# Two 3x3 convolutions of a metaformer block: where the batch statistics are taken, how the rectification is spread, and in which order three engines work in the second one

## The chip, the cores and the metric

The kernel runs on one core of a Trainium2 chip. The metric is the time of one execution on the device in microseconds (us). The core's engines work side by side, each through a queue of its own: TensorE (PE: matmuls), VectorE (DVE), ScalarE (ACT), GpSimd (POOL) and SyncE (SP, here only a queue for DMA). They wait for one another by semaphores. The two on-chip memories are SBUF and PSUM; matmuls write PSUM.

## The reference, cut to what matters

The program is a two-layer network on an image of 2 x 256 x 56 x 56 (batch, channels, rows, columns). Layer 0 is attention in windows and a mixture of experts. Layer 1 starts with this residual block of convolutions, and ends with a second mixture of experts. The change is in the block alone:

```python
def noised_tri_conv(x, w):
    tq = ternary_quantize(w - jnp.mean(w))          # -1, 0 or 1
    out = lax.conv_general_dilated(x, tq, (1, 1), ((1, 1), (1, 1)), ...)   # 3x3, 256 -> 256
    center = tq[:, :, 1, 1]
    return out + jnp.einsum('bchw,oc->bohw', x, center)

def batch_norm_train(x, gamma, beta):
    mean = jnp.mean(x, axis=(0, 2, 3), keepdims=True)
    var = jnp.var(x, axis=(0, 2, 3), keepdims=True)
    return (x - mean) * lax.rsqrt(var + BN_EPS) * gamma[...] + beta[...]

out1 = jax.nn.relu(batch_norm_train(noised_tri_conv(x, w1), g1, b1))
out2 = batch_norm_train(noised_tri_conv(out1, w2), g2, b2)
return jax.nn.relu(out1 + out2)
```

The mean and the variance go over the whole image of each channel. So nothing of `out1` can be rectified before the first convolution has ended everywhere, and nothing after the second can start before all its statistics are there.

## The kernel before, in words

**Tiling.** The image is cut into 14 strips of 8 rows (`STRIPS`, 7 per batch element; `SR` = 8, `NT` = 448 = 8 x 56). The channels lie on the 128 partitions in two halves (`KC` = 2; index `k` for the input's, `o` for the output's). `x_all` holds the results of all strips, `pad[b]` holds the padded input of one batch element, to which `inner(b, s)` and `narrow` give views.

**First convolution, `conv` (from line 1906).** It works on units of two strips. Rows are combined in pairs so that four products (`c`) with combined weights give two rows at once. `component(u, c)` makes the combined input `v` (VectorE for the first unit, GpSimd after it), ScalarE rounds it to `hi`, and VectorE makes the rest `lo = v - hi` (line 1903); both go through TensorE with the same weights, 12 matmuls of 448 columns for each `o` (line 1928). The results are summed into `x_all` by lines 1947 to 1954, and after the last product (c = 3) `bn_stats` takes the statistics of the two strips, one instruction each (line 1956).

**Affine.** `affine` aggregates the statistics with `bn_aggr` (line 2106) and makes a scale and a shift per channel. `between(i)` (line 2164 and around) rectifies strip i on ScalarE into `pad`, one instruction for each `o`.

**Second convolution, `conv43` (from line 1980).** It works on units of four strips, the first of two (`FOURS` = (0,1), (2-5), (6-9), (10-13)). Six products per unit (c = 0 to 5) give four rows at once. `component(u, c)` makes the combined input in PSUM (`pv`) out of helper tiles: p and q for c = 1 and 2, r and s for c = 3 and 4, a new r for c = 0, a new s for c = 5; r and s have one buffer each. For c = 3 the first unit makes r and s on VectorE, the later ones on GpSimd (`eng`, lines 2024 and 2025). ScalarE casts `hi` out of `pv` (line 2038) and VectorE makes `lo` (line 2039). A product has 12 matmuls for each `o` (line 2071), of 448 columns, of 224 in the first unit, into one of four PSUM banks (`pc`). ScalarE copies the results of c = 1 and 3 into `x_all` (line 2081), VectorE adds and subtracts those of c = 2 and 4 (lines 2084 and 2085), and adds those of c = 0 and 5 to rows 0 and 3 (lines 2087 and 2089). After c = 4, seven operations of GpSimd and ScalarE mix the four rows (lines 2093 to 2099: y0 += y2, y3 *= 2, y2 *= 3, y1 += y3, y2 += y0, y3 *= 3, y3 += y1). After c = 5, `bn_stats` takes the statistics strip by strip (line 2091), four instructions per `o`.

**What sets the order.** The order of the products is a list written out by hand (`steps`): (0,1) to (0,4), then for each next unit u: (u,1), (u-1,0), (u,2), (u-1,5), (u,3), (u,4); at the end (3,0), (3,5). In the source, the input of product n + 2 is made ahead of the matmuls of product n. `at_step` is called at the head of every product; `rectifying` then rectifies at c = 1 all strips of the next unit and one beyond, and strips 0 to 2 ahead of everything. Source order is the order on an engine only inside `tc.manual_schedule(engines=...)`. In `conv` that holds SP alone, in `conv43` no engine; there a planner in the compiler sets the order of each engine's queue from its own estimates. `ENGINES` is SP, DVE, PE and ACT, without POOL.

The next stage (`all_strips`, `residual`, from line 2203) needs scale2 and shift2.

Of the kernel before, what the change touches and what calls it, by code (L numbers as in the profile page):

```python
# [1 line left out]

# [1 line left out]

# [6 lines left out]
F32 = mybir.dt.float32  # L11
# [632 lines left out]
def metaformer(ctx: ExitStack, tc: tile.TileContext, a: dict, out: bass.AP, flag):  # L644
# [1199 lines left out]
    with mid:  # L1844

        with ExitStack() as st:
# [59 lines left out]
            def conv(sums, at_step):  # L1906
# [10 lines left out]
                for n, (u, c) in enumerate(steps):  # L1917
                    at_step(n)
                    if n + 2 < len(steps):
                        parts.append(component(*steps[n + 2]))  # L1920
                    hi, lo = parts.pop(0)
                    for o in range(KC):
                        pc = ps.tile([P, 512], F32, tag="cv", name="pc")
                        m = 0
                        for k in range(KC):
                            for dx in range(3):
                                for part in (hi, lo):
                                    nc.tensor.matmul(  # L1928
                                        pc[:, :NT],
                                        wq[:, k, c, dx * C + o * P : dx * C + (o + 1) * P],  # L1930
                                        part[:, :, k, dx : dx + W],
                                        start=m == 0,
                                        stop=m == 2 * KC * 3 - 1,
                                    )
                                    m += 1
                        pc = pc[:, :NT]

                        def row(y):
                            r = x_all[:, 2 * u : 2 * u + 2, o * NT : (o + 1) * NT]
                            r = r.rearrange("p s (h w) -> p s h w", w=W)[:, :, y : SR - 1 + y : 2, :]  # L1940
                            return r

                        def rows(ap):
                            return ap.rearrange("p (s h w) -> p s h w", s=2, w=W)

                        if c == 1:
                            nc.scalar.copy(row(1), rows(pc))
                        elif c == 2:
                            nc.vector.tensor_tensor(row(0), row(1), rows(pc), ALU.add)
                            nc.vector.tensor_tensor(row(1), row(1), rows(pc), ALU.subtract)  # L1950
                        elif c == 0:
                            nc.vector.tensor_tensor(row(0), row(0), rows(pc), ALU.add)
                        else:
                            nc.vector.tensor_tensor(row(1), row(1), rows(pc), ALU.subtract)
                            for i in (2 * u, 2 * u + 1):
                                nc.vector.bn_stats(stats[:, o, i, :], X[STRIPS[i]][:, o, :])
                return stats

            def weights43(taps):
# [20 lines left out]
            def conv43(wq, cp, vps, tp, at_step):  # L1980
# [6 lines left out]
                def component(u, c):  # L1987
# [7 lines left out]
                        else:  # L1995
                            runs.append([2 * (i - strips[0]), b, s * SR, 2])
                    n = 2 * len(strips)
                    eng = nc.gpsimd if u else nc.vector

                    def on_rows(op):  # L2000
                        for at, b, y, m in runs:
                            d = [pad[b][:, y + q : y + q + 4 * m - 3 : 4] for q in range(6)]
                            op(slice(at, at + m), d)
# [17 lines left out]
                        nc.vector.tensor_tensor(v, banks(p), banks(q), ALU.subtract)  # L2021
                    elif c == 3:
                        p, q = kept["r", u], kept["s", u] = tile_of("r", bufs=1), tile_of("s", bufs=1)
                        on_rows(lambda at, d: eng.tensor_tensor(p[:, at], d[4], d[2], ALU.subtract))
                        on_rows(lambda at, d: eng.tensor_tensor(q[:, at], d[3], d[1], ALU.subtract))
# [14 lines left out]
                    return hi, lo  # L2040

                stats = tp.tile([P, KC, len(STRIPS), 6], F32, tag="stats4", name="stats4")
                steps = [(0, c) for c in (1, 2, 3, 4)]
                for u in range(1, len(FOURS)):
                    steps += [(u, 1), (u - 1, 0), (u, 2), (u - 1, 5), (u, 3), (u, 4)]
                steps += [(len(FOURS) - 1, c) for c in (0, 5)]
                at_step(-1, 1)
                parts = [component(*steps[n]) for n in range(2)]
                for n, (u, c) in enumerate(steps):
# [8 lines left out]
                    def row(y, o):  # L2058
                        r = wide[:, :, o * NT : (o + 1) * NT]
                        return r.rearrange("p s (g q w) -> p s g q w", q=4, w=W)[:, :, :, y, :]  # L2060

                    def both(y):
                        return wide.rearrange("p s (g q w) -> p s g q w", q=4, w=W)[:, :, :, y, :]

                    for o in range(KC):
                        pc = ps.tile([P, 512], F32, tag="cv", name="pc")
                        m = 0
# [18 lines left out]
                        elif c == 0:  # L2086
                            nc.vector.tensor_tensor(row(0, o), row(0, o), got, ALU.add)
                        else:
                            nc.vector.tensor_tensor(row(3, o), row(3, o), got, ALU.add)
                            for i in strips:  # L2090
                                nc.vector.bn_stats(stats[:, o, i, :], X[STRIPS[i]][:, o, :])
                    if c == 4:
                        nc.gpsimd.tensor_tensor(both(0), both(0), both(2), ALU.add)
                        nc.scalar.mul(both(3), both(3), 2.0)
                        nc.scalar.mul(both(2), both(2), 3.0)
                        nc.gpsimd.tensor_tensor(both(1), both(1), both(3), ALU.add)
                        nc.gpsimd.tensor_tensor(both(2), both(2), both(0), ALU.add)
                        nc.scalar.mul(both(3), both(3), 3.0)
                        nc.gpsimd.tensor_tensor(both(3), both(3), both(1), ALU.add)
                return stats  # L2100

            def affine(stats, g, beta, tp, eps=eps5):

                mv = tp.tile([P, KC, 2], F32, tag="mv", name="mv")
                for o in range(KC):
                    nc.vector.bn_aggr(mv[:, o, :], stats[:, o].rearrange("p s c -> p (s c)"))
# [44 lines left out]

            with tc.manual_schedule(engines={mybir.EngineType.SP}):
                stats = conv(sums[0], combining)
            scale, shift = affine(stats, bn["g1"], bn["b1"], rp)
# [4 lines left out]
            def between(i):  # L2159
# [3 lines left out]
                for o in range(KC):  # L2163
# [17 lines left out]
        wq_held.close()  # L2181

        with ExitStack() as both:
# [335 lines left out]
```

## Time and profile before

| what | value |
|---|---|
| time, median of 3 runs | 1740.41 us (1736.08 to 1745.44) |
| time of the profiled execution | 1737.13 us |
| its span in the trace | 1735.3 us |
| busy in the span | PE 87%, DVE 55%, ACT 40%, POOL 37% |
| first convolution, matmuls of line 1928 start | 817.6 to 994.9 us |
| second convolution, matmuls of line 2071 start | 1004.6 to 1129.0 us |
| first transposes of the next stage | 1137.8 us |

Engines in three stretches (busy us; "clock" is the TensorE clock that was granted, as a share of full speed):

| stretch, us | PE | DVE | ACT | POOL | clock |
|---|---|---|---|---|---|
| 1025 to 1052 | 27.0 | 25.9 | 9.0 | 10.1 | 0.98 |
| 1052 to 1084 | 31.3 | 25.5 | 9.8 | 13.8 | 1.00 |
| 1084 to 1129 | 41.4 | 31.5 | 12.6 | 20.6 | 1.00 |

How to read the lines of the profile: a line of the timeline has the start in us, the duration in us, engine, line of the code, operation, output <- inputs with partitions x elements, and how many were merged; in brackets the engine's idle time before it and what ended it. A line of a group has line, engine, operation, count | busy us, mean ns | idle time before, and what ended most of it. "PE busy" counts a matmul from start to modelled end; as matmuls overlap, the time that one takes from the engine is read from the distance between starts.

### The profile page before, as it was taken

Reading aid. Unit: us, or ns where it says so; the run is one execution under the profiler, and the core shown is the slowest. Engines: PE = TensorE matmul, PEld = TensorE weight load, DVE = VectorE, ACT = ScalarE, POOL = GpSimd, SP = SyncE. Lnnn points to the kernel's source line nnn. Section 1 sums busy time; section 2 is a strip of 40 time slices with the busy share of each in tenths; the row PEclk is TensorE's granted clock in tenths of the full one; section 3 lists DMA queues with packets and bytes.
Section 4 is the critical chain, followed back from the end, with each engine's and each line's share of the span. In section 5 each row is a group of like instructions: output and inputs, shape, how many; then the busy total and the mean of one; then the engine's idle time right before and its main releaser. Section 6 shows DMA issues by size and latency. Waiting matters only on the chain. (4 is left out here: it accounts for less than half of the span.)

```text
span 1735.3 us, 25573 instructions
## 1 busy us (share of the span) xinstructions
PE 1507.6 (87%) x8445; PEld 1176.0 (68%) x8445; DVE 957.5 (55%) x2620; ACT 692.9 (40%) x1419; POOL 636.8 (37%) x728
## 2 busy tenths in 40 slices
PE   5999998999878788894989879957769999999964
PEld 3555565556557667783768768746658888888852
DVE  3456667466635335885999888777622212111136
ACT  2544443444323324544444263235423334343323
POOL 2111436235333653552333323427715542222210
PEclk9999999999879999996999989955579999999975
DMA  7112334112257769794441000024357777888858
GB/s 241 42 64 90 111 102 145 60 62 80 80 181 248 249 203 322 258 331 176 170 170 70 1 1 0 10 65 141 126 198 274 271 258 262 282 288 288 293 198 317
DMA packets 94157, 291.78 MB, mean 168 GB/s; under 512 B 20151, under 2 KB 35611, under 8 KB 84928
## 3 DMA queue, kind: packets, MB, share of 16 engines
q1 hardware_dynamic: 70384, 231.82, 40.3%
q0 software_dynamic: 19824, 51.82, 7.9%
q10 hardware_dynamic: 3808, 6.42, 1.0%
q8 instruction: 69, 1.13, 0.3%
q14 instruction: 72, 0.59, 0.1%
HBM read 218.55 MB, written 74.20 MB: 169 GB/s over the span
## 5 line engine op out<-in xcount | busy, mean ns | idle before, releaser
L1187 PE MATMUL ph<-ut,w 128*128 128x256 f32 (+1 forms) x1472 | 311.8, 363 | 18.5 <-DMA w<-in_L_experts 10.0
L1216 DVE TENSOR_TENSOR y<-py,w 128x512 f32<-128x512 f32 (+1 forms) x120 | 76.8, 640 | 412.5 <-PE py L1206 341.4
L1206 PE MATMUL py<-w,h 128*128 128x256 f32 x1288 | 300.5, 381 | 3.4 <-DVE y L1216 2.5
L1187 PEld LDWEIGHTS ph<-ut,w 128*128 128x128 f32 x1472 | 251.4, 195 | 49.6 <-DMA w<-in_L_experts 10.3
L1206 PEld LDWEIGHTS py<-w,h 128*128 128x128 f32 x1288 | 244.5, 192 | 37.1 <-DVE y L1216 2.9
L934 POOL DMA_INDIRECT xs<-u,pos x196 | 194.0, 990 | 127.9 <-issue 43.1
L1218 POOL DMA_INDIRECT ys<-y,dest x136 | 137.0, 1008 | 233.0 <-DVE dest L1162 100.4
L1194 ACT ACTIVATE h<-ph,w 128x256 f32<-128x256 f32 (+1 forms) x368 | 162.6, 448 | 119.0 <-PE ph L1187 91.5
L1597 ACT ACTIVATE ex<-sc 112x476 f32<-112x476 f32 (+3 forms) x224 | 116.9, 573 | 177.6 <-PE sc L1587 169.8
L1159 ACT COPY ut<-pt 128x512 f32<-128x512 f32 (+1 forms) x120 | 65.1, 543 | 293.1 <-PE pt L1155 258.2
L1928 PE MATMUL pc<-lo,wq 128*128 128x448 f32 x336 | 131.8, 394 | 5.7 <-DVE lo L1903 5.4
L1617 DVE TENSOR_TENSOR acc<-av,acc 128x238 f32<-128x238 f32 (+3 forms) x224 | 88.1, 408 | 82.9 <-PE av L1607 74.7
L1928 PE MATMUL pc<-hi,wq 128*128 128x448 f32 x336 | 131.0, 392 | 2.5 <-DVE x L1950 1.9
L1607 PE MATMUL av<-ex,vals 112*64 112x238 f32 (+3 forms) x896 | 126.9, 407 | 4.0 <-DVE acc L1617 4.0
L1218 POOL DMA_INDIRECT ys<-y,to x81 | 81.7, 1009 | 121.9 <-DVE dest L1162 63.4
L2071 PE MATMUL pc<-hi,wq 128*128 128x448 f32 (+1 forms) x288 | 102.5, 366 | 18.1 <-ACT hi L2038 9.4
L1578 PE MATMUL sc<-q_im,keys 32*112 32x238 f32 (+3 forms) x896 | 99.2, 423 | 7.9 <-ACT ex L1597 7.8
L2071 PE MATMUL pc<-lo,wq 128*128 128x448 f32 (+1 forms) x288 | 101.8, 363 | 0.2 <-DVE lo L2039 0.2
L1155 PE MATMUL pt<-ident,xg 128*128 128x128 f32 x434 | 71.2, 285 | 33.6 <-DMA xg<-xs 25.5
L1901 POOL TENSOR_TENSOR v<-pad 128x928 f32<-128x928 f32 (+1 forms) x28 | 56.7, 2035 | 103.5 <-ACT pad L1884 59.5
L1607 PEld LDWEIGHTS av<-ex,vals 112*64 112x64 f32 x896 | 57.3, 143 | 53.5 <-issue 30.0
L1155 PEld LDWEIGHTS pt<-ident,xg 128*128 128x128 f32 x434 | 56.5, 148 | 48.8 <-DMA xg<-xs 22.5
(278 smaller groups left out, 2474.5 us busy)
## 6 DMA issues: line engine op xcount, KB each, us to landing
w<-in_L_experts SPq DMA_DIRECT2D x64, 1154.0 KB
w<-in_L_experts SPq DMA_DIRECT2D x56, 641.0 KB
xg<-xs SPq DMA_DIRECT2D x97, 260.0 KB
acc<-in_fresh SPq DMA_DIRECT2D x14, 896.0 KB
got<-ys SPq DMA_DIRECT2D x21, 512.0 KB
got<-ys SPq DMA_DIRECT2D x7, 1024.0 KB
xt<-in_x_tok SPq DMA_DIRECT2D x14, 448.0 KB
rec<-shares SPq DMA_DIRECT2D x28, 224.0 KB
```

The source lines that it names most:

```text
L934: w = nc.gpsimd.indirect_dma_start(xs[:, :], bass.IndirectOffsetOnAxis(ap=pos[:, j, t0 + t : t0 + t + 1], axis=0), at_of[t][0][:, at_of[t] ...
L1155: nc.tensor.transpose(pt[:, k, i * P : (i + 1) * P], d["xg"][:, i, k * P : (k + 1) * P], ident)
L1187: nc.tensor.matmul(ph[:, :g], w1[:, k, f * P : (f + 1) * P], d["ut"][:, k, :g], start=k == 0, stop=k == KC - 1,)
L1194: nc.scalar.activation(d["h"][:, f, :g], ph[:, :g], AF.Gelu, bias=b1[:, f : f + 1])
L1206: nc.tensor.matmul(py[:, i, :], d["h"][:, f, i * P : (i + 1) * P], w2[:, f, :], start=f == 0, stop=f == NF - 1,)
L1218: o = nc.gpsimd.indirect_dma_start(ys[:, :], bass.IndirectOffsetOnAxis(ap=d["to"][:, i : i + 1], axis=0), y[:, i, :], None, bounds_check=T ...
L1578: nc.tensor.matmul(sc[h // 2][:, h % 2, :nq], keys[g][p, c, tx * TT : (tx + 1) * TT], q_im[p, c, r0:r1, c0:c1], start=True, stop=False,)
L1597: nc.scalar.activation(e[:, :, :nq], sc[j][:, :, :nq], AF.Exp, scale=HD**-0.5)
L1607: nc.tensor.matmul(av[VW * i : VW * (i + 1), :nq], vals[g % 3][:, tx, 2 * c + j, 2 * i : 2 * i + 2, :].rearrange("p a d -> p (a d)"), ex[j ...
L1617: added = nc.vector.tensor_tensor(d, av[:, :nq].rearrange("p (h w) -> p h w", w=c1 - c0), d, ALU.add)
L1928: nc.tensor.matmul(pc[:, :NT], wq[:, k, c, dx * C + o * P : dx * C + (o + 1) * P], part[:, :, k, dx : dx + W], start=m == 0, stop=m == 2 * ...
L2071: nc.tensor.matmul(pc[:, : 2 * ns * W], wq[:, k, c, dx * C + o * P : dx * C + (o + 1) * P], part[:, : 2 * ns, k, dx : dx + W], start=m == ...
```

## The change

It has five parts.
1. In `conv`, the statistics are taken of the even and of the odd rows of a unit instead of its two strips; those of the even rows stand ahead of the last subtraction.
2. In `conv43` they are taken by rows too: rows 0, 1 and 2 of all groups of four (in the two-strip unit the first two rows) stand ahead of the last addition, the rest behind it. After the last unit each `o` is aggregated at once; `affine` is handed the aggregates.
3. `rectifying` rectifies one strip at the head of each product instead of a unit's strips together.
4. `conv43` stands in `manual_schedule(engines=ENGINES)`, so VectorE, TensorE and ScalarE work in source order there (the function has no SP instruction). GpSimd's queue is the planner's as before.
5. The mix after c = 4 becomes a generator, `mixed`, whose parts are written behind the following two products. In the last unit rows 1 and 3 are summed on VectorE, in two times four operations, the other two on GpSimd. The first unit's r and s go to GpSimd.

```diff
@@ conv
                         else:
+                            nc.vector.bn_stats(stats[:, o, 2 * u, :], row(0))
                             nc.vector.tensor_tensor(row(1), row(1), rows(pc), ALU.subtract)
-                            for i in (2 * u, 2 * u + 1):
-                                nc.vector.bn_stats(stats[:, o, i, :], X[STRIPS[i]][:, o, :])
+                            nc.vector.bn_stats(stats[:, o, 2 * u + 1, :], row(1))
@@ conv43
-                    eng = nc.gpsimd if u else nc.vector
...
-                        on_rows(lambda at, d: eng.tensor_tensor(p[:, at], d[4], d[2], ALU.subtract))
-                        on_rows(lambda at, d: eng.tensor_tensor(q[:, at], d[3], d[1], ALU.subtract))
+                        on_rows(lambda at, d: nc.gpsimd.tensor_tensor(p[:, at], d[4], d[2], ALU.subtract))
+                        on_rows(lambda at, d: nc.gpsimd.tensor_tensor(q[:, at], d[3], d[1], ALU.subtract))
...
+                mv = tp.tile([P, KC, 2], F32, tag="mv4", name="mv4")
...
+                def mixed(y, ns, last):
+
+                    nc.gpsimd.tensor_tensor(y[0], y[0], y[2], ALU.add)
+                    if last:
+                        for i in range(ns):
+                            nc.vector.scalar_tensor_tensor(
+                                y[1][:, i], y[3][:, i], 2.0, y[1][:, i], ALU.mult, ALU.add
+                            )
+                        for i in range(ns):
+                            nc.vector.scalar_tensor_tensor(
+                                y[3][:, i], y[3][:, i], 6.0, y[1][:, i], ALU.mult, ALU.add
+                            )
+                        nc.scalar.mul(y[2], y[2], 3.0)
+                        nc.gpsimd.tensor_tensor(y[2], y[2], y[0], ALU.add)
+                        yield
+                        return
+                    nc.scalar.mul(y[3], y[3], 2.0)
+                    yield
+                    nc.scalar.mul(y[2], y[2], 3.0)
+                    nc.gpsimd.tensor_tensor(y[1], y[1], y[3], ALU.add)
+                    nc.gpsimd.tensor_tensor(y[2], y[2], y[0], ALU.add)
+                    yield
+                    nc.scalar.mul(y[3], y[3], 3.0)
+                    nc.gpsimd.tensor_tensor(y[3], y[3], y[1], ALU.add)
+
+                mixing = iter(())
...
+                    def pair_of(y):
+
+                        def rows_y(o):
+                            r = wide[:, :, o * NT : (o + 1) * NT]
+                            r = r.rearrange("p s (g r) -> p s g r", g=2)
+                            return r[:, :, :, y * 2 * W : (y + 1) * 2 * W]
+
+                        return rows_y
...
+                    if ns == 2:
+                        parts_of = [pair_of(y) for y in range(2)]
+                    else:
+                        parts_of = [partial(row, y) for y in range(4)]
...
                         else:
+                            for at, y in enumerate(parts_of[:-1]):
+                                nc.vector.bn_stats(stats[:, o, strips[at], :], y(o))
                             nc.vector.tensor_tensor(row(3, o), row(3, o), got, ALU.add)
-                            for i in strips:
-                                nc.vector.bn_stats(stats[:, o, i, :], X[STRIPS[i]][:, o, :])
+                            nc.vector.bn_stats(stats[:, o, strips[-1], :], parts_of[-1](o))
+                            if u == len(FOURS) - 1:
+                                all_of(mv, stats, o)
+                    next(mixing, None)
                     if c == 4:
-                        nc.gpsimd.tensor_tensor(both(0), both(0), both(2), ALU.add)
...
-                        nc.gpsimd.tensor_tensor(both(3), both(3), both(1), ALU.add)
-                return stats
...
+                        mixing = mixed([both(y) for y in range(4)], ns, u == len(FOURS) - 1)
+                        next(mixing)
+                return mv
+
+            def all_of(mv, stats, o):
+                nc.vector.bn_aggr(mv[:, o, :], stats[:, o].rearrange("p s c -> p (s c)"))
...
+            waiting = list(range(3, len(STRIPS)))
+
             def rectifying(u, c):
-                if c == 1 and u + 1 < len(FOURS):
-                    if u < 0:
-                        between(0)
-                    for i in FOURS[u + 1]:
-                        between(i + 1)
-
-            stats = conv43(wq4[0], cp, vps, rp, rectifying)
-            scale2, shift2 = affine(stats, bn["g2"], bn["b2"], rt, eps5_36)
+                if u < 0:
+                    for i in range(3):
+                        between(i)
+                elif waiting and (u or waiting[0] <= FOURS[1][-1] + 1):
+                    between(waiting.pop(0))
+
+            with tc.manual_schedule(engines=ENGINES):
+                mv = conv43(wq4[0], cp, vps, rp, rectifying)
+            scale2, shift2 = affine(mv, bn["g2"], bn["b2"], rt, eps5_36)
```

More of the change, by code (lines that the diff above doesn't have):

```diff
@@ L1 @@
 from contextlib import ExitStack, nullcontext
+from functools import partial
 import numpy as np
@@ L2088, in conv43, with affine @@
                         else:
+                            for at, y in enumerate(parts_of[:-1]):
+                                nc.vector.bn_stats(stats[:, o, strips[at], :], y(o))
                             nc.vector.tensor_tensor(row(3, o), row(3, o), got, ALU.add)
-                            for i in strips:
-                                nc.vector.bn_stats(stats[:, o, i, :], X[STRIPS[i]][:, o, :])
+                            nc.vector.bn_stats(stats[:, o, strips[-1], :], parts_of[-1](o))
+                            if u == len(FOURS) - 1:
+                                all_of(mv, stats, o)
+                    next(mixing, None)
                     if c == 4:
-                        nc.gpsimd.tensor_tensor(both(0), both(0), both(2), ALU.add)
[L2094 to L2099, printed above, removed]
-                return stats
[L2102 to L2106, printed above, removed]
+                        mixing = mixed([both(y) for y in range(4)], ns, u == len(FOURS) - 1)
[3 more added lines that the diff above has]
+                nc.vector.bn_aggr(mv[:, o, :], stats[:, o].rearrange("p s c -> p (s c)"))
+            def affine(mv, g, beta, tp, eps=eps5):
                 scale = tp.tile([P, KC], F32, tag="scale", name="scale")
@@ L2153, in metaformer @@
                 stats = conv(sums[0], combining)
-            scale, shift = affine(stats, bn["g1"], bn["b1"], rp)
+            mv = rp.tile([P, KC, 2], F32, tag="mv", name="mv")
+            for o in range(KC):
+                all_of(mv, stats, o)
+            scale, shift = affine(mv, bn["g1"], bn["b1"], rp)
             first_on.close()
```

## The prediction, on record before the changed kernel ran

> **What bounds the stage now.** I read the page first (TensorE busy 87% of the span), then the windows of the second convolution (its matmuls start from 1004.6 to 1129.0 us), then TensorE's groups there, then the timelines of VectorE, ScalarE and GpSimd one under the other. Successive matmuls of 448 columns start 0.2165 us apart (1117.41, 1117.63, 1117.85), those of 224 columns 0.1115 us. So 432 and 144 of them need 93.5 + 16.1 = 109.6 us. The stage takes 124.8 us: TensorE bounds it, and some 15 us are waits and slow clock. TensorE's groups say where:
>
> ```profile
> L2071 PE MATMUL pc<-hi,wq 128*128 128x448 f32 x216 | 82.2, 381 | 4.2 <-ACT x L2081 2.2 <-DVE x L2085 1.9
> L2071 PE MATMUL pc<-hi,wq 128*128 128x224 f32 x72 | 20.4, 320 | 13.9 <-ACT hi L2038 9.4 <-DVE x L2085 3.5 <-ACT x L2081 1.0
> ```
>
> 9.4 us is the first input after the first convolution's statistics. The 3.5 us (from 1016.5 to 1020.0) comes while ScalarE runs seven rectifications in a row from 1014.72; after it matmuls of 224 columns start 0.214 us apart, half pace, until 1025.2. Few waits are left to win in the three large units.
>
> VectorE keeps up only because the planner put other work between `pv` and the `lo` made from it:
>
> ```profile
> 1071.54 1.13 DVE L2018 TENSOR_TENSOR pv<-p,q 128x928 f32<-128x928 f32 x1
> 1072.58 0.61 DVE L2085 TENSOR_TENSOR x<-x,pc 128x448 f32<-128x448 f32 x1
> 1073.11 0.61 DVE L2084 TENSOR_TENSOR x<-x,pc 128x448 f32<-128x448 f32 x1
> 1073.64 1.12 DVE L2039 TENSOR_TENSOR lo<-pv,hi 128x928 fp32r<-128x928 f32 x1
> 1074.67 0.61 DVE L2085 TENSOR_TENSOR x<-x,pc 128x448 f32<-128x448 f32 x1
> ```
> ```profile
> 1072.78 0.93 ACT L2038 CAST hi<-pv 128x928 fp32r<-128x928 f32 x1 [3.45 <-DVE pv L2018]
> ```
>
> ScalarE's `hi` starts 1.24 us after `pv` started; after a `hi`, `lo` starts 0.97 us later (1098.84 to 1099.81). Back to back, `lo` would start 2.21 us after `pv`, where the queue could have gone on after 1.04. Here two additions fill the gap.
>
> **Second convolution, large units.** From starts on VectorE's timeline, a unit of four strips costs it: 16 operations of 928 elements in six components at 1.04 = 16.6 us; four pairs of additions (2.38 for two pairs, 1039.56 to 1041.94) 4.8; four single additions at 0.53, 2.1; eight statistics at 0.53, 4.2. Sum 27.7 us, against TensorE's 144 x 0.2165 = 31.2. The change puts VectorE into source order, and the source has `lo` right behind `pv`. Behind each waiting `lo` stand the evacuations of the running product, for which TensorE's four result banks wait. Six waits of 2.21 - 1.04 = 1.17 are 7.0 us; with 0.3 for operations that follow their own input, 35.0. VectorE becomes the bound.
>
> To this come collisions with GpSimd:
>
> ```profile
> 1092.51 2.10 POOL L2097 TENSOR_TENSOR x<-x 128x896 f32<-128x896 f32 x1
> 1094.57 2.97 POOL L2096 TENSOR_TENSOR x<-x 128x896 f32<-128x896 f32 x1
> ```
> ```profile
> 1092.59 3.02 DVE L2006 SCALAR_TENSOR_TENSOR pv<-s,r 128x928 f32<-128x928 f32 x1 [2.60 <-POOL s L2025]
> ```
>
> The same `pv` takes 1.13 us at 1101.38; here it ends 2 us late, as if it had stood until GpSimd's operation ended, and GpSimd's next, 2.11 elsewhere, stretches in turn. The Trainium skill (SBUF — State Buffer, "Who interferes with whom") states it as a rule: a VectorE instruction with two SBUF inputs contends with a GpSimd instruction that reads SBUF, and the one that comes second blocks for the whole of it. The rows agree, also in that `lo` (one input in PSUM) keeps 1.12 us at 1088.87 beside GpSimd's work. Today, late operations of this kind sum to some 8 us in the stage. In source order their place is fixed: GpSimd's sum of rows 0 and 2 starts after the additions of c = 4 and meets the next `pv`, rows 1 and 2 meet c = 5's `pv`, row 3 meets c = 3's `pv`: waits of about 1.5, 2.0 and 1.3, 4.8 us a unit. By the rows without the rule (collisions fall into waits that are there anyway) a unit costs 35.0; with it, 39.8. I take 39.8.
>
> I laid the source order out in this way, operation behind operation with these durations, and for a check laid out the order of before likewise: it ends its last aggregate at 1135.3, where the trace has 1135.4. The products compared:
>
> - Start to (1,1). The three leading strips are six rectifications of 0.667 us, as now. The first unit's r and s move to GpSimd: no row has 464 elements there; 448 take 1.15, 696 take 1.69; I take 1.3. Its r holds up the first `pv`, so TensorE starts 0.6 us later than now. But with one strip per product no seven rectifications stand ahead of a `hi`: the 3.5 us and the second half-pace period go. (1,1) starts at 1019.4 instead of 1025.2: -5.8 us. At r and s of 1.15 or 1.7 this moves by under 1 us. The later strips' rectifications, 1.33 us a product, run on ScalarE mostly while VectorE makes the next `pv`; where they hold up a `hi` (by 1.9 us before (0,4), less after), it is in these figures.
> - (1,1) to (2,1), with the first unit's last two half-size products: 31.0 instead of 26.4 us, +4.6.
> - (2,1) to (3,1): a whole large unit, 39.8 instead of 32.1, +7.7.
> - (3,1) to the additions of (3,4): another such unit, with VectorE's queue some 6 us behind TensorE by then; 46.1 instead of 37.5, +8.6.
>
> **The tail.** Now the statistics stand behind GpSimd's and ScalarE's alternating chain:
>
> ```profile
> 1128.98 0.62 DVE L2089 TENSOR_TENSOR x<-x,pc 128x448 f32<-128x448 f32 x1 [0.93 <-POOL x L2099]
> 1129.64 2.21 DVE L2091 BATCH_NORM_STATS2 stats<-x 128x6 f32<-128x448 f32 x4
> 1131.76 0.60 DVE L2089 TENSOR_TENSOR x<-x,pc 128x448 f32<-128x448 f32 x1
> 1132.28 0.53 DVE L2106 BATCH_NORM_AGGREGATE mv<-stats 128x2 f32<-128x84 f32 x1
> 1132.73 2.14 DVE L2091 BATCH_NORM_STATS2 stats<-x 128x6 f32<-128x448 f32 x4
> ```
>
> From the additions of (3,4) (1121.2) to the last aggregate (1135.4) it is 14.2 us. The change does rows 1 and 3 on VectorE in eight operations of 224 elements; its operations on 232 elements start 0.31 us apart, so 2.5 us. They have two SBUF inputs and meet GpSimd's two sums, 1.5 + 2.0 us of waiting. Then two additions 1.1, and per half three statistics, addition, statistic, aggregate: 3.2, twice. Sum 13.5: -0.8. Row statistics would let TensorE's end be followed by 1.7 us only, if VectorE were on time; it is not. Without the collisions the tail gains 4.3.
>
> **First convolution.** Statistics of even rows move ahead of the last subtraction: one statistic less between the last matmul and the aggregates, -0.5. Same count, same elements; a strided statistic has no row here, bounded at no more and double (0.53), the latter +0.5 at the tail; I take no more, since the additions on such strided rows and the statistics on plain ones both take 0.53 us now. Elsewhere TensorE or other VectorE work covers it. Splitting the aggregates into a helper costs nothing. No DMA is moved: the changed functions issue none.
>
> **Sum.** -0.5 - 5.8 + 4.6 + 7.7 + 8.6 - 0.8 = +13.8. What follows (from 1137.8) hangs on the scale and shift and shifts whole. Against the profiled execution, 1737.13 us (span 1735.3), that is 1751; that execution lies 3.3 under the median, so against 1740.41 I predict 1754.
>
> **Rivals.** A measurement here can tell about 0.5% (8.7 us) from no change, so "same" is 1731.7 to 1749.1.
> - Collisions mostly fall into waits: units cost 35.0. By the same layout the stage ends at 1135, no change: about 1740. For: GpSimd is free to be ordered by the planner, and two of its operations per unit (r and s) do start as `hi` is awaited. Against: the 3.02 us row.
> - Faster: the waits for `hi` don't bind, because VectorE's queue is not really that of the source, or is early enough. Then TensorE decides: start 1004.6, 109.6 us, 2.5 for the first half-pace product, 1.9 of tail: 1118.6, so -17 and about 1724. It decides where VectorE's unit, 27.7 plus waits, stays under 31.2, so at waits under 3.5 us; six of 1.17 speak against, and the chance is what I leave for misreading the order.
> - GpSimd's queue puts r and s of the next unit behind the mix: c = 3 then waits for both, laid out 12 us worse: 1766.
>
> **Chances.** Main case 0.50 (1747 to 1762, the lowest end of it "same"), collisions hidden 0.22, faster 0.14, GpSimd late 0.14. Faster by over 0.5%: 0.14; within 0.5%: 0.26; slower 0.60. The range leaves out the faster case and the outer part of the last: 1734 to 1767.
>
> **What would show it.** Right: in the changed trace VectorE waits about 1.1 us for ScalarE's `hi` before nearly every `lo` (24 of them, over 20 us), TensorE's idle time in the large units is put down to VectorE, products (2,1) to (3,1) lie near 40 us apart, the 3.5 us wait and the second half-pace period are gone, the last aggregate comes 9 us after TensorE's end. Wrong: `lo` not next to `pv`, a unit near 32 us, or pairs like that at 1092 gone.

## The result, and the profile after

The changed kernel takes 1751.89 us (median of 9 runs, 1748.94 to 1761.71), the kernel before 1740.41 (9 runs, 1735.97 to 1747.26). The ratio is 1.0072, with an interval of 1.0054 to 1.0091: slower by 9 to 16 us. The profiled execution of after took 1752.7 us with a span of 1750.9, 15.6 more than that of before; the mean clock is 0.899 in both.

The stage from the first scale (the square root on ScalarE, L2109 before, L2148 after) to the second is where the time is: 137.8 us before (997.68 to 1135.47), 152.7 after (1001.49 to 1154.20), +14.9. The first convolution, from its first matmul to its shift (the last of the four small operations that VectorE does with the scale; it starts at 998.59 before and 1002.40 after), went from 181.0 to 179.5. The remaining 2.2 us of the span's 15.6 can't be put down to the change: the first convolution starts 5.3 us later (822.9 instead of 817.6), and what follows the second scale is 3.1 us shorter. In the twelve profiled executions of this study, with the same code ahead of it, that start lies anywhere between 815.3 and 830.3. So the experiments below are read by the stage's length, each from one trace, and by ratios of many runs, never by absolute times of one trace.

The stage by its parts, against the forecast (a product is dated by the start of its first matmul):

| part | before | forecast | after |
|---|---|---|---|
| shift of the first to first matmul | 6.0 | 6.6 | 7.3 |
| shift of the first to (1,1) | 26.6 | 20.8 | 21.6 |
| (1,1) to (2,1) | 26.4 | 31.0 | 30.9 |
| (2,1) to (3,1) | 32.1 | 39.8 | 39.7 |
| (3,1) to the additions of (3,4) | 37.5 | 46.1 | 46.05 |
| those additions to the last aggregate | 14.2 | 13.5 | 13.5 |

VectorE's timeline in the second unit shows both costs of the source order, one behind the other. The first figure of a line is the start, the second the duration; in brackets is the idle time before it and what ended it:

```profile
1062.27 2.62 DVE L2021 TENSOR_TENSOR pv<-p,q 128x928 f32<-128x928 f32 x1
1065.97 1.13 DVE L2039 TENSOR_TENSOR lo<-pv,hi 128x928 fp32r<-128x928 f32 x1 [1.08 <-ACT hi L2038]
1067.01 1.11 DVE L2006 SCALAR_TENSOR_TENSOR s<-pad 128x928 f32<-128x928 f32 x1
1068.16 2.93 DVE L2037 TENSOR_TENSOR pv<-s,q 128x928 f32<-128x928 f32 x1
1072.14 1.12 DVE L2039 TENSOR_TENSOR lo<-pv,hi 128x928 fp32r<-128x928 f32 x1 [1.06 <-ACT hi L2038]
```

GpSimd's timeline over the same microseconds:

```profile
1061.78 2.12 POOL L2050 TENSOR_TENSOR x<-x 128x896 f32<-128x896 f32 x1 [1.58 <-DVE x L2124]
1063.86 3.00 POOL L2067 TENSOR_TENSOR x<-x 128x896 f32<-128x896 f32 x1
1067.73 2.37 POOL L2068 TENSOR_TENSOR x<-x 128x896 f32<-128x896 f32 x1 [0.88 <-ACT x L2066]
1071.17 2.33 POOL L2025 TENSOR_TENSOR s<-pad 128x232 f32<-128x232 f32 x2 [1.07 <-DVE pv L2037]
```

And ScalarE's two conversions:

```profile
1065.00 0.94 ACT L2038 CAST hi<-pv 128x928 fp32r<-128x928 f32 x1 [0.34 <-DVE pv L2021]
...
1071.18 0.94 ACT L2038 CAST hi<-pv 128x928 fp32r<-128x928 f32 x1 [2.22 <-DVE pv L2037]
```

`lo` now stands right behind its `pv`, so VectorE idles until `hi` is written. Each `pv` starts just after one of GpSimd's sums has started, and ends 1.0 us after that sum ends (1064.89 against 1063.90, 1071.09 against 1070.10): as if it had waited for the sum and then done its work, 2.62 and 2.93 us on the record for work that takes 1.12. GpSimd's next sum waits in turn and stretches to 3.00. By the two effects five operations of 1.04 us take 10.9 us here (1062.27 to 1073.18).

The waits between 1000 and 1150 us (total, times, longest) add up the first effect, and show where TensorE pays. The first line is VectorE's, the others TensorE's:

```profile
DVE lo L2039 <- ACT hi L2038: 24.6, 23, 2.8
...
PE pc L2111 <- ACT x L2121: 6.3, 4, 2.5
PE pc L2111 <- DVE x L2125: 3.7, 4, 2.0
PE pc L2111 <- DVE x L2127: 3.0, 2, 1.6
PE pc L2111 <- DVE x L2131: 2.2, 2, 1.1
```

TensorE's waits here are for evacuations of its banks: L2125, L2127 and L2131 are VectorE's additions, queued behind the waiting `lo`. Those put down to L2121, ScalarE's copies, lead back to VectorE too: the copies stand in ScalarE's queue behind a `hi`, and that waits for a `pv` that comes late in VectorE's queue. Ahead of (3,1), for one, `pv` starts at 1091.96, `hi` at 1093.20, the copies at 1094.03, the matmul at 1094.62, 2.5 us after TensorE ran dry.

The tail has the same marks (VectorE after the additions of (3,4)):

```profile
1140.71 2.64 DVE L2053 SCALAR_TENSOR_TENSOR x<-x 128x224 f32<-128x224 f32 x4
1143.28 3.20 DVE L2057 SCALAR_TENSOR_TENSOR x<-x 128x224 f32<-128x224 f32 x4
1146.40 1.14 DVE L2127 TENSOR_TENSOR x<-x,pc 128x448 f32<-128x448 f32 x2
```

The eight sums on VectorE take 5.7 us (1140.71 to 1146.40) beside GpSimd's two, and the rest of the queue stands behind them, up to the last aggregate, which ends at 1154.16.

### The profile page after: what moved, and what is told of

Its sections match the earlier page's. It is cut to its first block, busy times and chain, and to the rows that moved or that the text cites. A ratio compares the mean times of both kernels' runs of the same rounds, so it can differ in the third digit from the quotient of the medians.

```text
span 1750.9 us, 25579 instructions
## 1 busy us (share of the span) xinstructions
PE 1510.2 (86%) x8445; PEld 1176.0 (67%) x8445; DVE 967.6 (55%) x2626; ACT 691.4 (39%) x1417; POOL 634.6 (36%) x728
## 5 line engine op out<-in xcount | busy, mean ns | idle before, releaser
L1188 PE MATMUL ph<-ut,w 128*128 128x256 f32 (+1 forms) x1472 | 310.5, 362 | 16.2 <-DMA w<-in_L_experts 10.7
```

The source lines that it names most:

```text
L1188: nc.tensor.matmul(ph[:, :g], w1[:, k, f * P : (f + 1) * P], d["ut"][:, k, :g], start=k == 0, stop=k == KC - 1,)
```

## The experiments

Theory: source order on VectorE costs the time, by waits for `hi` and by collisions with the mix on GpSimd. Rivals: another part of the change (row statistics, spread rectifications, the shared last sums, r and s on GpSimd) costs it; or one of the two effects lies hidden in the other. "Stage" is scale to scale, 137.8 us before and 152.7 after. Times are medians, ratios are to the kernel before on the same chip. The orders of VectorE and of TensorE were not undone one by one; that VectorE's is what costs is read from the waits and from e2 and e3.

| kernel | stage, us | time, us | ratio, interval |
|---|---|---|---|
| e1_planner | 134.2 | 1735.84 | 0.9985, 0.9963 to 1.0007 |
| e2_lo_late | 141.8 | 1742.71 | 1.0024, 1.0004 to 1.0043 |
| e3_no_mix | 135.7 | 1736.85 | 0.9983, 0.9966 to 1.0000 |
| e4_before_source_order | 162.6 | 1764.84 | 1.0144, 1.0104 to 1.0183 |
| e5_act_order | 136.0 | 1737.51 | 0.9986, 0.9971 to 1.0001 |
| e6_act_order_rs | 135.3 | 1733.29 | 0.9955, 0.9934 to 0.9976 |
| e7_last_mix_as_before | 152.7 | 1755.67, one run | - |
| e8_rs_vector | 151.1 | 1752.87, one run | - |
| e9_no_mix_lo_late | 134.9 | 1736.82, one run | - |
| e10_mix_vector | 128.7 | 1727.52 | 0.9917, 0.9894 to 0.9941 |

### e1_planner: the change without the order

```diff
-            with tc.manual_schedule(engines=ENGINES):
+            with nullcontext():
                 mv = conv43(wq4[0], cp, vps, rp, rectifying)
```

> The changed kernel with the source order undone: the second convolution is left to the planner on every engine, all other parts of the change stay. Main theory (the loss is VectorE's waits for hi and the places of the collisions, both set by the source order): the second convolution, from the first scale to the last aggregate, falls from 151.6 us to under the 136.7 of the kernel before, by the tail and the rectifications that are no longer in a row: 122 to 132, and the time is 1725 to 1737, faster than the 1740 of before. Rival (the other parts of the change cost as such: row statistics, first unit's r and s on GpSimd, split mix): it stays at 1747 to 1753.

The stage is 134.2 us, 18.5 less than after: the order costs all that was lost, and the rest of the change does no harm. The stage is 3.6 less than before, which the time can't tell from no change. It falls short of what was expected (122 to 132, counted from the first rectification to the last aggregate; so counted it is 133.1), and that the kernel is faster than before isn't shown. One loss lies at the head. The planner put rectifications in a row on ScalarE again, though the source spreads them, and a `hi` stands behind five of them:

```profile
1018.53 3.39 ACT L2206 ACTIVATE pad<-x,shift,scale 128x448 f32<-128x448 f32 x5
1021.81 0.52 ACT L2038 CAST hi<-pv 128x464 fp32r<-128x464 f32 x1
```

VectorE waits 2.54 us for it. Soon after come the two parts of p, which take 1.18 us elsewhere, beside GpSimd's r:

```profile
1022.37 0.64 DVE L2039 TENSOR_TENSOR lo<-pv,hi 128x464 fp32r<-128x464 f32 x1 [2.54 <-ACT hi L2038]
...
1023.73 3.15 DVE L2006 SCALAR_TENSOR_TENSOR p<-pad 128x232 f32<-128x232 f32 x2
```
```profile
1023.86 2.27 POOL L2024 TENSOR_TENSOR r<-pad 128x928 f32<-128x928 f32 x1 [12.71 <-DVE pv L2033]
```

The additions that free TensorE's banks stand behind both. TensorE's timeline shows the price, the same wait as before the change and half pace again (0.21 apart instead of 0.11, at a granted clock of 0.50 from 1026.37 to 1033.19):

```profile
1027.74 0.53 PE L2111 MATMUL pc<-hi,wq 128*128 128x224 f32 x1 [3.51 <-DVE x L2125]
1028.07 0.41 PE L2111 MATMUL pc<-lo,wq 128*128 128x224 f32 x1
```

### e4_before_source_order: the order alone

```diff
-            stats = conv43(wq4[0], cp, vps, rp, rectifying)
+            with tc.manual_schedule(engines=ENGINES):
+                stats = conv43(wq4[0], cp, vps, rp, rectifying)
```
The kernel before, and nothing else of the change.

> The kernel before with one part of the change alone: the second convolution in source order on VectorE, TensorE, ScalarE. Main theory: this part is the whole loss, and the rest of the change wins some of it back: laid out in the same way, the last aggregate comes 26 us later than in the kernel before, so 1760 to 1770, slower than the changed kernel. Rival (the order costs little and the other parts cost): 1740 to 1748.

The stage is 162.6 us, +24.8. Here VectorE's waits between 1000 and 1150 us, with the rectifications of a unit still together ahead of a `hi`, are:

```profile
DVE lo L2039 <- ACT hi L2038: 40.5, 23, 7.7
```

So the order costs the kernel before 25 us, and the rest of the change wins 9.9 of them back (162.6 to 152.7). Up to the end of the stage, at 1171.6, the waits are 41.5 us in 24 times; they fall to 24.6 once the rectifications are spread, which is where most of it probably comes from. A part may be TensorE's clock: in its units e4 had five periods at a granted clock of 0.50, 23.9 us together, the changed kernel two of 3.4.

### e2_lo_late: the order without the wait

```diff
-                    nc.vector.tensor_tensor(banks(lo), v, banks(hi).bitcast(F32), ALU.subtract)
+                    late.append(
+                        lambda: nc.vector.tensor_tensor(
+                            banks(lo), v, banks(hi).bitcast(F32), ALU.subtract
+                        )
+                    )
...
                     if n + 2 < len(steps):
                         parts.append(component(*steps[n + 2]))
+                    if late:
+                        late.pop(0)()
```

> The changed kernel in source order, with one move: lo of an input is issued on VectorE behind the next input's pv, not right behind its own. Main theory: the waits of some 1.07 us for hi ahead of 23 lo (24.6 us in the changed trace) are gone, the collisions with GpSimd stay or grow a little (some 20 us), so the last aggregate comes 8 to 14 us earlier and the time is 1738 to 1744. If the waits for hi were all of the loss: over 20 us earlier, under 1732. If TensorE or ScalarE set the pace in truth: no change, 1750.

The stage is 11.0 us shorter than after, as expected, and the waits for `hi` are gone from VectorE. Two things remain. TensorE now waits for `lo` itself:

```profile
PE pc L2119 <- DVE lo L2041: 15.5, 8, 3.6
```

And a collision's other half appears: VectorE, early now, waits for the mix to let go of a row.

```profile
1059.61 1.12 DVE L2041 TENSOR_TENSOR lo<-pv,hi 128x928 fp32r<-128x928 f32 x1
1064.28 1.15 DVE L2135 TENSOR_TENSOR x<-x,pc 128x448 f32<-128x448 f32 x2 [3.55 <-POOL x L2073]
```

### e3_no_mix: the order without GpSimd's sums

```diff
-                    if c == 4:
-                        mixing = mixed([both(y) for y in range(4)], ns, u == len(FOURS) - 1)
-                        next(mixing)
```

> The changed kernel with the mix after c = 4 left out (the sums and products of the four rows on GpSimd, ScalarE and, in the last unit, VectorE; the output rows are then not those of the convolution). The waits for hi stay, the collisions of VectorE with the mix go. Main theory: a large unit costs 35 us instead of 39.8, the last unit's eight sums (5.7 us) go too, so the last aggregate comes 16 to 20 us earlier: 1732 to 1736. Rival (collisions fall into waits that are there anyway): only the eight sums of the last unit count, 5 to 7 us, 1745 to 1747.

This leaves out ScalarE's products too. The stage is 17.0 us shorter than after (16 to 20 expected; the time, 1736.85, is just above the 1732 to 1736 expected). Of this, 5.7 are the last unit's eight sums on VectorE, left out as well. The other 11 go with the mix and, by the lines, with its collisions: from (2,1) to (3,1) it is 35.3 us instead of 39.7, and the 4.4 saved match what the three late operations of that unit had lost (1.5, 1.8 and 1.2). `pv` takes 1.12 us again, at the same place in the order, while the wait for `hi` stands (between 1000 and 1150 us, VectorE waited 25.3 us for it in 24 waits):

```profile
1058.77 1.12 DVE L2021 TENSOR_TENSOR pv<-p,q 128x928 f32<-128x928 f32 x1
1060.97 1.12 DVE L2039 TENSOR_TENSOR lo<-pv,hi 128x928 fp32r<-128x928 f32 x1 [1.08 <-ACT hi L2038]
1062.02 1.11 DVE L2006 SCALAR_TENSOR_TENSOR s<-pad 128x928 f32<-128x928 f32 x1
1063.16 1.13 DVE L2037 TENSOR_TENSOR pv<-s,q 128x928 f32<-128x928 f32 x1
```

The rival "collisions hidden in waits" put a unit at 35.0 us with the mix in place; the kernel comes near that only when the mix is gone.

### e9_no_mix_lo_late: both at once

It has the edits of e2 and e3.

> The changed kernel in source order with both suspected costs taken away: lo behind the next input's pv, and the mix after c = 4 left out (its output rows are then not those of the convolution). If the two are the whole loss, TensorE bounds the stage again: from first scale to second 8.2 us to the first matmul, 109.6 us of matmuls, 2.5 for the half-pace start, some 2 to 4 of waits, 3 at the end: 125 to 131 us. If something else holds the stage (ScalarE's order, TensorE's waits for result banks), it stays at 134 or more.

The stage is 134.9 us: together the two bring 17.8, not 11.0 + 17.0. That is the 134 or more that was expected if something else holds the stage: a third limit stands behind them. VectorE's waits show what kind it is:

```profile
DVE x L2135 <- PE pc L2119: 11.0, 8, 2.0
DVE x L2132 <- PE pc L2119: 9.2, 9, 1.3
DVE x L2132 <- ACT pad L2211: 4.5, 1, 4.5
```

VectorE waits for products while TensorE waits for `lo` (10.7 us on its weight loads, in 6 waits). So each waits in its fixed order for something that the other will finish later; that work which it could do stood queued behind is likely, but not shown by these lines. How much of this is the place that I gave `lo`, and how much would remain in any fixed order, these runs don't settle.

### e5_act_order and e6_act_order_rs: order on ScalarE alone

```diff
-            with tc.manual_schedule(engines=ENGINES):
+            with tc.manual_schedule(engines={mybir.EngineType.Activation}):
                 mv = conv43(wq4[0], cp, vps, rp, rectifying)
```

> The changed kernel with source order on ScalarE alone in the second convolution; VectorE, TensorE and GpSimd are left to the planner. In the run with the planner on all engines ScalarE had 5 and 8 rectifications in a row and TensorE lost 3.5 us plus a half-pace period again. Main theory (source order costs on VectorE and pays on ScalarE, where it keeps the rectifications spread): from the first scale to the second the stage takes 126 to 132 us against 134.2 with the planner on all and 152.7 in the changed kernel; time 1727 to 1735. Rival (source order costs on whichever engine has it, because hi now stands behind copies and rectifications): 135 to 142 us, 1737 to 1745.

Here an order is set for ScalarE only, and VectorE is left to the planner. The 3.5 us wait is gone (TensorE's longest wait in the units is 1.7). VectorE even waits longer than in e1 for the same `hi`, 3.84 us, but p no longer meets r there. The stage is 136.0 us, not the 126 to 132 that I expected; stage and time (1737.51) lie in the range of the rival, that the order costs on whichever engine has it. Up to TensorE's end it doesn't: its last matmul comes 128.3 us after the scale (129.4 in e1). What is won is lost on VectorE: its additions of (3,4) end 122.6 us after the scale (120.8 in e1), and from there to the last aggregate it is 13.4 us in both. Its waits for `hi` are 7.7 us (4.5 in e1), those of statistics for GpSimd's rows 5.4 (6.6 in e1); what puts it 1.8 us behind stays open. By their times e5 and e1 are the same.

e6 also gives the first unit's r and s back to VectorE:

```diff
+                    eng = nc.gpsimd if u else nc.vector
...
-                        on_rows(lambda at, d: nc.gpsimd.tensor_tensor(p[:, at], d[4], d[2], ALU.subtract))
-                        on_rows(lambda at, d: nc.gpsimd.tensor_tensor(q[:, at], d[3], d[1], ALU.subtract))
+                        on_rows(lambda at, d: eng.tensor_tensor(p[:, at], d[4], d[2], ALU.subtract))
+                        on_rows(lambda at, d: eng.tensor_tensor(q[:, at], d[3], d[1], ALU.subtract))
```

> As the run with source order on ScalarE alone, and the first unit's r and s back on VectorE. In the changed kernel they run on GpSimd just as VectorE makes p, q and pv for the first product, and each of q and pv ends 0.9 us late. Main theory: TensorE's first matmul comes 1 to 1.4 us earlier after the scale (6.9 us instead of 8.2), and the stage is shorter by that and no more, 1726 to 1734. Rival (the planner's new order outweighs it): the start moves, the stage end doesn't.

The first matmul comes 6.9 us after the scale instead of 8.2, but the stage is only 0.7 us shorter than e5's. The kernel is the first that is faster than before, by 0.2 to 0.7%; that its median lies 4.2 us under e5's is more than the stage of one trace accounts for. Its VectorE shows that the planner doesn't avoid the collisions either:

```profile
1098.24 2.25 DVE L2007 SCALAR_TENSOR_TENSOR s<-pad 128x696 f32<-128x696 f32 x1
1100.53 2.92 DVE L2038 TENSOR_TENSOR pv<-s,q 128x928 f32<-128x928 f32 x1
...
1105.74 3.02 DVE L2007 SCALAR_TENSOR_TENSOR pv<-s,r 128x928 f32<-128x928 f32 x1 [0.74 <-POOL s L2026]
```

### e7_last_mix_as_before and e8_rs_vector: two small parts, undone alone

e7 runs the last unit's mix as the other units' (`mixed(..., False)`, drained at once); e8 makes the edit of e6 in the changed kernel, with its order on three engines.

> The changed kernel, in source order, with the last unit's mix on GpSimd and ScalarE as in the other units instead of shared with VectorE. Main theory (the eight sums on VectorE take 5.7 us with their collisions, GpSimd's chain 4 x 2.1 us and runs beside VectorE's statistics): from first scale to second the stage changes by less than 1.5 us either way. Rival (sharing is what shortens the tail): 4 us longer or more.

> The changed kernel, in source order, with the first unit's r and s back on VectorE. Main theory: q and pv of the first product are no longer late, first matmul 1 to 1.4 us earlier after the scale (6.9 us instead of 8.2); two operations of 0.55 us more on VectorE for c = 3 of the first unit; the stage ends 0 to 1.3 us earlier. Rival: no change of the start.

e7's stage is 152.7 us, as long as after's: sharing the last sums brings nothing. In e7 VectorE waits 5.68 us for GpSimd's sum at the place where in the changed kernel its eight sums take 5.7 with their collisions. e8's first matmul comes 6.4 us after the scale instead of 8.2, and its stage is 1.6 us shorter, a little more than expected. The changed kernel's start shows why (VectorE, then GpSimd):

```profile
1005.35 0.64 DVE L2006 SCALAR_TENSOR_TENSOR p<-pad 128x464 f32<-128x464 f32 x1 [2.79 <-ACT pad L2206]
1005.91 1.60 DVE L2006 SCALAR_TENSOR_TENSOR q<-pad 128x464 f32<-128x464 f32 x1
1007.55 1.49 DVE L2018 TENSOR_TENSOR pv<-p,q 128x464 f32<-128x464 f32 x1
```
```profile
1005.40 1.62 POOL L2024 TENSOR_TENSOR r<-pad 128x464 f32<-128x464 f32 x1 [21.11 <-ACT pad L2206]
1006.98 1.56 POOL L2025 TENSOR_TENSOR s<-pad 128x464 f32<-128x464 f32 x1
```

q and `pv`, operations of 0.64 us, end 0.5 us after r and s (1007.02 and 1008.54): each is late by a collision.

### e10_mix_vector: no mix on GpSimd at all

On top of e6, the whole mix runs on VectorE, with ScalarE's multiplications folded in:

```diff
+                    nc.vector.tensor_tensor(y[0], y[0], y[2], ALU.add)
+                    for at, src, by, add in ((1, 3, 2.0, 1), (3, 3, 6.0, 1), (2, 2, 3.0, 0)):
+                        for i in range(ns):
+                            nc.vector.scalar_tensor_tensor(
+                                y[at][:, i], y[src][:, i], by, y[add][:, i], ALU.mult, ALU.add
+                            )
+                    yield
```

> Source order on ScalarE alone, first unit's r and s on VectorE (as in the fastest run so far), and the whole mix on VectorE: one addition and twelve operations of 224 elements per unit, about 4.8 us, in place of GpSimd's four sums and ScalarE's three products. In that run VectorE's operations with two SBUF inputs ended 6.9 us late in the third unit (2.88, 2.25, 2.92, 3.02, 1.47 us instead of about 1.1). Main theory: doing the sums on VectorE costs less than colliding with them, 2 us a unit, so the stage is 131 to 134 us instead of 135.3 and the time 1727 to 1733. Rival: VectorE is the bound, and 4.8 us of own work per unit weigh more than collisions that partly lie in waits: 137 to 142 us, over 1735.

The stage is 128.7 us, better than expected (131 to 134), and the time 1727.52: 0.6 to 1.1% faster than before. VectorE takes on 4.6 us a unit:

```profile
1076.94 1.08 DVE L2051 TENSOR_TENSOR x<-x 128x896 f32<-128x896 f32 x1
1077.94 3.70 DVE L2054 SCALAR_TENSOR_TENSOR x<-x 128x224 f32<-128x224 f32 x12
1081.56 1.12 DVE L2022 TENSOR_TENSOR pv<-p,q 128x928 f32<-128x928 f32 x1
```

That is about what the collisions took from it in the changed kernel (4.5 us in the second unit). TensorE's waits for VectorE sum to 3.6 us from 1000 us on. Of the 6.6 us that the stage is shorter than e6's, 3.8 lie ahead of TensorE's last matmul and 2.8 behind it. The edit also ends the handing to and fro between GpSimd and ScalarE in the mix; what that is worth, and whether this kernel still needs the order on ScalarE, wasn't tried.

## Why the prediction was right

- **The waits for `hi`.** Forecast were 24 of 1.17 us; 23 with a total of 24.6 came, 1.07 on average. The step's place was right too: additions stand behind the waiting `lo`, and TensorE waits for those. e2 shows it, by 11.0 us.
- **The collisions.** Forecast were 1.5, 2.0 and 1.3 us a unit in the three places where sums of GpSimd start ahead of a `pv`; those at 1062, 1068 and 1074 are 1.5, 1.8 and 1.2 late, and thirteen operations over the stage are late by 0.75 to 1.9, some 16 us together. The sum taken with the rule of exclusion (the Trainium skill, SBUF — State Buffer, "Who interferes with whom"), 39.8 us a unit, agrees with the measured 39.7, and the one without it, 35.0, does not; in e3 the same `pv` at the same place takes 1.12 us.
- **The start.** That (1,1) comes 5.8 us sooner was 5.0. The first matmul is 1.3 us later than before, not 0.6 (e8 gives it back): r no longer stands ahead of `pv` on VectorE, 0.55 us, but q and `pv` are 0.96 and 0.85 late, two collisions where the forecast had one wait. The 3.5 us wait and the half-pace period behind it went, as forecast, but the reason given was wrong. The prediction puts the wait down to seven rectifications in a row. TensorE waited for an addition on VectorE (L2085), and the lines of before show what stood ahead of the additions:

```profile
1014.63 0.64 DVE L2039 TENSOR_TENSOR lo<-pv,hi 128x464 fp32r<-128x464 f32 x1 [2.58 <-ACT hi L2038]
...
1015.99 3.15 DVE L2006 SCALAR_TENSOR_TENSOR p<-pad 128x232 f32<-128x232 f32 x2
1019.06 0.37 DVE L2084 TENSOR_TENSOR x<-x,pc 128x224 f32<-128x224 f32 x1
```
```profile
1016.12 2.27 POOL L2024 TENSOR_TENSOR r<-pad 128x928 f32<-128x928 f32 x1 [35.08 <-DVE pv L2033]
```

It is a wait for a `hi` behind five earlier rectifications (1010.78 to 1014.18), and then a collision of p with GpSimd's r, 2 us. The seven held up only the next `hi`, of (1,1). In the changed kernel VectorE waits for the same `hi` still longer, but the additions come next:

```profile
1017.37 0.64 DVE L2039 TENSOR_TENSOR lo<-pv,hi 128x464 fp32r<-128x464 f32 x1 [2.84 <-ACT hi L2038]
1017.93 0.38 DVE L2124 TENSOR_TENSOR x<-x,pc 128x224 f32<-128x224 f32 x1
```

So the size came out right because the forecast laid out VectorE's order, in which the additions stand ahead of p; that the stated reason, of which the trace shows no part, pointed the same way was luck. The planner's runs bear this out: e5, with 3.84 us for the `hi` and no collision, has TensorE waiting 1.7 us, and e1, with 2.54 us and the collision, 3.5.
- **The tail.** 13.5 us as forecast, with eight sums of 5.7 where 2.5 + 3.5 was forecast. e7 confirms that sharing them is worth nothing beside collisions. The last aggregate ends 8.4 us after TensorE, 9 by the forecast.
- **The first convolution.** Forecast -0.5, measured -1.5. From the last subtraction's start to the shift it went from 3.33 us (995.26 to 998.59) to 2.80 (999.60 to 1002.40): the forecast 0.5. A statistic on every second row takes 0.63 us, as one on plain rows does. The other 1.0 may be no more than the spread between traces: from the first matmul to the scale it is 176.4 to 179.1 us in the ten with the changed code, 180.1 and 182.6 in the two with the old.
- **The sum.** +13.8 was forecast for the span. The stage and the first convolution give 14.9 - 1.5 = +13.4; the medians of nine runs each differ by 11.5, with 9 to 16 in the interval; 1754 was predicted for the median of 1751.89.
- **The rivals.** e3 and the measured unit speak against hidden collisions, VectorE's waits against a faster kernel. GpSimd's r and s did not come late: r runs ahead of the mix (1057.88 against 1061.78) and s ahead of its last sum (1071.17 against 1073.45), and VectorE waited 0.4 us for one s in the whole stage.

What the forecast did not see is that its two effects aren't independent: each undone alone brings 11 and 17 us, both 17.8 (e9).

## What to carry to other kernels

An operation of an in-order queue that needs another engine's answer to the operation just ahead costs the round trip each time, here 1.07 us, and everything behind it pays; before fixing an order, look in the trace at what stands between the two. Here an order on ScalarE alone cost nothing that the times show (ratio 0.9986, and 0.9985 with no order), the order on three engines 0.7%. Lay the fixed order out with the durations of the trace, collisions included: here that gave the stage's parts to within a microsecond. When TensorE waits, follow the operation that ended the wait back through its engine's queue; what another engine did at the same time need not be the cause. And work moved to an idle GpSimd isn't free while VectorE runs operations with two SBUF inputs beside it: here the same sums cost less on the full VectorE.

## What the hardware showed besides

- Half pace doesn't need one long wait, and a longer wait doesn't always bring it. In the changed kernel the granted clock was 0.50 from 1096.39 to 1099.80, after 2.89 us without a start, and from 1133.94 to 1137.35, after 1.86 us (1131.40 to 1133.26). In the kernel before it stayed at 1.00 after 2.55 us (1096.44 to 1098.99). Matmuls of 448 columns start 0.37 us apart at 0.50, and 0.216 otherwise:

```profile
1091.73 0.37 PE L2111 MATMUL pc<-lo,wq 128*128 128x448 f32 x1
1094.62 0.48 PE L2111 MATMUL pc<-hi,wq 128*128 128x448 f32 x1 [2.52 <-ACT x L2121]
...
1096.62 0.57 PE L2111 MATMUL pc<-hi,wq 128*128 128x448 f32 x1
1097.00 0.57 PE L2111 MATMUL pc<-lo,wq 128*128 128x448 f32 x1
```

The places show a pattern. In each of the twelve traces all changes of the clock within the stage lie whole multiples of 3.41 us apart (here 1014.47, 1096.39, 1099.80, 1133.94, 1137.35). Cut on that grid, the pieces of the twelve stages at full clock sort by TensorE's busy share in the profile: under 0.46, all 21 were followed by a piece at 0.50; from 0.47 to 0.54, 3 of 12; above, none. The two pieces ahead of the changed kernel's half-pace periods have 0.45 and 0.51; the wait of before is split between pieces of 0.76 and 0.61. The two periods didn't show in the stage's parts, which came as forecast without them.

- r and s of the first unit, 464 elements, take 1.62 and 1.56 us on GpSimd, where 448 take 1.15. But r starts while p runs on VectorE and s while q does; from the ends of these (1005.99 and 1007.51) each takes 1.03 us. So the collision costs both sides, and 464 elements as such are not slow.
- An operation of VectorE that writes to PSUM collides as one that writes to SBUF does, if both its inputs are in SBUF: `pv`, which lies in PSUM, took 2.62 and 2.93 us instead of 1.12, and q, in SBUF, 1.60 instead of 0.64.
